# Seven block products in place of eight for the query, key and first feed-forward projections of a graph network layer

## The chip, the cores and the metric

The kernel runs on one NeuronCore of a Trainium2 chip. The metric is the device time of one launch in microseconds. Five engines of the core matter here: TensorE (PE in the profile, with PEld for its weight loads), VectorE (DVE), ScalarE (ACT), GpSimd (POOL) and SyncE (SP), which only issues DMAs. Each engine works through its own list of instructions in order and waits on semaphores for the others. Matrix products land in PSUM, which has eight banks of 512 float32 values per partition; everything else lies in SBUF.

## The reference

The input is x, 128 graphs of 64 nodes with 256 features, all in float32, and one 64x64 adjacency matrix. Four layers are added to x one after the other, each on a normalised copy of x with a ReLU. Layer 0 is a graph convolution followed by LSTMs over windows of 1 to 4 nodes. Layer 2 is graph attention, and layer 3 works in the eigenbasis of a graph Laplacian. Layer 1 is the one that the change touches:

```python
xp = jnp.einsum('mn,bnf->bmf', L_norm, x)
h = jax.nn.relu(_layernorm(xp @ Wc + bc, g1, be1))
x1 = h + x
q, k, v = x1 @ Wq, x1 @ Wk, x1 @ Wv          # 256 x 256 each, then split into 4 heads
attn = softmax(where(adjacency > 0, q @ k.T / sqrt(hd), -1e9))
o = (attn @ v) @ Wo + bo
x2 = _layernorm(x1 + o, g2, be2)
m = jax.nn.gelu(x2 @ W1 + b1) @ W2 + b2      # W1 is 256 x 512
return _layernorm(x2 + m, g3, be3)
```

(The listing is shortened: the reshapes into heads are left out.)

## The kernel before

The 8192 tokens (128 graphs of 64 nodes) are worked on as 64 tiles of 128 tokens. Layer 0 takes them in 8 groups of 8 tiles and writes its result to a buffer in HBM. Layers 1 to 3 take them in 16 groups of 4 tiles, so 512 tokens at a time: each group is fetched, goes through layer1, layer2 and layer3 (lines 1485, 1560, 1594), and is written to the output. Beside layer 0, an eigendecomposition of the 64x64 Laplacian runs, nearly all of it on VectorE.

The program text doesn't issue instructions. Every engine call is recorded by a planner (class Plan, lines 69 to 345), which sorts all recorded operations into one order by list scheduling on costs of its own, gives each value a buffer from a pool (36 "big" buffers of 1024 values per partition in the end, 8 PSUM banks, and smaller ones), and then issues everything from line 344. That is why every line of the profile says L344: instructions are told apart by the names of their tiles, which here are names of pools. In layers 1 to 3 "Wih" and "Whh" in a name are no LSTM weights: the room of LSTM weights that are done with is given to the weights of the later layers.

Three properties of the planner bear on the change. Groups overlap: up to 8 groups of layers 1 to 3 may be under way, and the operation of an older group mostly goes first; the last six groups count as one, and there the operation with the longest path behind it goes first (rank, line 328). A matrix product that depends on another engine is planned no earlier than 0.4 us after its inputs are expected (slack, line 976), 0.12 us for layer 0. VectorE's operations on SBUF alone and GpSimd's operations are planned never to overlap (the variable port in schedule, line 227). Dependences are taken from regions of a buffer, so two halves of a bank count as independent; the framework under it that inserts the semaphores decides for itself.

Weights of layers 1 to 3 are loaded once, as group WEIGHTS, when the last group of layer 0 lets go of the LSTM weights: a Carver (line 899) hands out the columns of these tiles first come, first served (lines 1390 to 1423).

In layer1, to_fm (line 1436) transposes x1 so that features lie on partitions: x1T is 128 partitions by 2 chunks of features by 512 tokens. proj_fm (line 1443) makes one half (128) of the output features of a projection: two products of 128x128 weights with 512 tokens, added up in one PSUM bank. Query and key take two calls each, W1 takes four. Their results are copied out of PSUM by evac (line 1430, VectorE for an even number, ScalarE for an odd one), and for W1 by ScalarE's Gelu with its bias. The value, Wc, Wo and W2 projections go through proj_tm (line 1449) and have 256 columns.

Products by seven block products exist already for the LSTM: pieces (line 1245) makes four differences of the blocks of the moving operand, the combinations of the weight blocks are prepared once (lines 1076 to 1088), and lstm_fast (line 1261) adds up the seven products with three PSUM banks.

Of the kernel before, what the change touches and what calls it, by code (L numbers as in the profile page):

```python
# [8 lines left out]
ALU = mybir.AluOpType  # L9
AF = mybir.ActivationFunctionType  # L10
# [877 lines left out]
P = 128  # L888
D = 256
# [3 lines left out]
HT = 4  # L893
# [39 lines left out]
def gnn_kernel(ctx: ExitStack, tc: tile.TileContext, a, out):  # L933
# [4 lines left out]
    def C(shape, name):  # L938
        return pool.tile(list(shape), F32, name=name)
# [3 lines left out]
    wih = [C([P, 2 * (3 if p == 0 else 4) * D], f"Wih{p}") for p in range(4)]  # L943
    whh = [None] + [C([P, 8 * D], f"Whh{p}") for p in range(1, 4)]
# [36 lines left out]
    plan = Plan(tc, {"PE": nc.tensor, "V": nc.vector, "ACT": nc.scalar, "G": nc.gpsimd, "SP": nc.sync}, pools, late, reserve, window, EIG, REST + NT // HT - 6, slack)  # L981
    PE, V, ACT, G, SP = (plan.proxy(e) for e in ("PE", "V", "ACT", "G", "SP"))

    def bank(name):
        return plan.value("bank")

    def load(t, src):
        SP.dma_start(t, src)
        return t

    def chunks(src):
        return src.rearrange("(c p) f -> p c f", p=P)
# [25 lines left out]
    Wg = [load(C([P, 2, D], f"Wg{i}"), chunks(a[f"Wg{i}"])) for i in range(2)]  # L1018
# [48 lines left out]
    B1T = C([P, 2, 2, P], "B1T")  # L1067
# [10 lines left out]
    for p in (1, 2):  # L1078
        fastw[p] = []
        for i, w in enumerate((Wih[p], Whh[p])):  # L1080
            a11, a12, a21, a22 = (w.rearrange("p k (q m n) -> p k q m n", q=4, m=2)[:, k, :, m, :] for m in range(2) for k in range(2))
            s1, s2, s4 = (space.tile([P, 4, P]) for j in range(3))
            s3 = a21 if i else space.tile([P, 4, P])
# [21 lines left out]
    room = Carver(arena)  # L1105
# [53 lines left out]
    flat = lambda t: t.rearrange("p t f -> p (t f)")  # L1159
# [21 lines left out]
    def fm():  # L1181

        return plan.value("big")[:, :2 * HT * P].rearrange("p (c n) -> p c n", c=2)
# [4 lines left out]
    def transposes(srcs):  # L1188

        pt = bank("tr")  # L1190
        for i, s in enumerate(srcs):
            PE.transpose(pt[:, i * P:(i + 1) * P], s, ident)
        return pt
# [51 lines left out]
    def pieces(B, eng):  # L1245

        n = B(0, 0).shape
        w = 1
        for k in n[1:]:
            w *= k  # L1250
        t = plan.value("big")[:, :4 * w].rearrange("p (i n) -> p i n", i=4)
        t = [t[:, i] for i in range(4)]
        if len(n) == 3:
            t = [v.rearrange("p (w t) -> p w t", t=n[2]) for v in t]
        eng.tensor_tensor(t[0], B(0, 1), B(0, 0), op=ALU.subtract)
        eng.tensor_tensor(t[1], B(1, 1), t[0], op=ALU.subtract)
        eng.tensor_tensor(t[2], B(1, 1), B(0, 1), op=ALU.subtract)
        eng.tensor_tensor(t[3], B(1, 0), t[1], op=ALU.subtract)
        return {1: B(0, 0), 2: B(1, 0), 3: B(1, 1), 4: t[3], 5: t[0], 6: t[1], 7: t[2]}
# [128 lines left out]


    plan.group = WEIGHTS  # L1390
    room = Carver(wih[1], whh[1], wih[2], whh[2], wih[0])
    wtile = lambda src: load(room.tile([P, src.shape[0] // P, src.shape[1]]), chunks(src))
    btile = lambda src, n=D: load(room.tile([P, n]), src.to_broadcast([P, n]))
    ctile = lambda shape, src: load(room.tile(shape), src)
    Wc, Wq, Wk, Wv, W1, W2, Wo = (wtile(a[n]) for n in ("Wc", "Wq", "Wk", "Wv", "W1", "W2", "Wo"))
    bc, g1, be1, bo, g2, be2, b2, g3, be3 = (btile(a[n]) for n in ("bc", "g1", "be1", "bo", "g2", "be2", "b2", "g3", "be3"))
    b1 = ctile([P, 4], a["b1"])

    g2c, be2c = (ctile([P, 2], a[n].rearrange("o (c p) -> p (o c)", p=P)) for n in ("g2", "be2"))
    G.tensor_tensor(b2, b2, be2, op=ALU.add)  # L1400
    W2a = wtile(a["L2_W"])

    wa = room.tile([P, 2, D])
    WT, a12 = fm(), wtile(a["L2_a"])
# [25 lines left out]
    def evac(dst, src, i):  # L1430
        if i % 2:
            ACT.copy(dst, src)
        else:
            V.tensor_copy(dst, src)
# [8 lines left out]
    def proj_fm(w, src, m):  # L1443
        ps = bank("fm")
        for c in range(2):
            PE.matmul(ps, w[:, c, tok(m)], src[:, c, :], start=c == 0, stop=c == 1)
        return ps

    def proj_tm(lhs, w, nk, t0):

        ps = bank("tm")
        for t in range(2):
            for c in range(nk):
                PE.matmul(ps[:, t * D:(t + 1) * D], lhs(c, t0 + t), w[:, c, :], start=c == 0, stop=c == nk - 1)
        return ps
# [29 lines left out]
    def layer1(x):  # L1485
        h = relu_norm(x)
        lx = mix_fm(h, lambda t: lapb)
        x1 = tm()
        for t0 in (0, 2):
            ps = proj_tm(lambda c, t: lx[:, c, tok(t)], Wc, 2, t0)  # L1490
            V.tensor_add(x1[:, t0:t0 + 2, :], ps.rearrange("p (t f) -> p t f", t=2), vec(bc, 2))
        norm(x1)
        for t0 in (0, 2):
            xp, hp = x1[:, t0:t0 + 2, :], h[:, t0:t0 + 2, :]
            V.tensor_mul(xp, xp, vec(g1, 2))
            G.tensor_add(xp, xp, vec(be1, 2))
            V.scalar_tensor_tensor(xp, xp, 0.0, hp, op0=ALU.max, op1=ALU.add)
        x1T = to_fm(x1)
        qT, kT, v = fm(), fm(), tm()
        for m in range(2):  # L1500
            evac(qT[:, m, :], proj_fm(Wq, x1T, m), 0)
            evac(kT[:, m, :], proj_fm(Wk, x1T, m), 1)
        for t0 in (0, 2):
            evac(pair(v, t0), proj_tm(lambda c, t: x1T[:, c, tok(t)], Wv, 2, t0), 1)
        for t0 in (0, 2):
            G.tensor_add(x1[:, t0:t0 + 2, :], x1[:, t0:t0 + 2, :], vec(bo, 2))


        ps = [bank("qk") for m in range(2)]
        with plan.burst():  # L1510
            for b, m, r in [(b, m, r) for b in range(2 * HT) for m in range(2) for r in range(2)]:
                PE.matmul(ps[m][half(r ^ m), bat(b)], qT[half(r), m, bat(b)], kT[half(r), m, bat(b)], start=True, stop=True)
        s = tm(4 * HT, N)
        for m in range(2):
            sm = s[:, m * 2 * HT:(m + 1) * 2 * HT, :]
            V.scalar_tensor_tensor(sm, ps[m].rearrange("p (b k) -> p b k", k=N), 0.125, vec(mask1, 2 * HT), op0=ALU.mult, op1=ALU.add)
            stat = plan.value("stat")
            softmax_shift(sm, stat[:, :2 * HT])
            ACT.activation(sm, sm, AF.Exp)
            ssum = stat[:, 2 * HT:4 * HT]  # L1520
            V.reduce_sum(ssum, sm, axis=AX.X)
            V.reciprocal(ssum, ssum)
            G.tensor_mul(sm, sm, ssum.unsqueeze(2).to_broadcast([P, 2 * HT, N]))

        pT = fm()
        for m in range(2):
            evac(pT[:, m, :], transposes([flat(s[:, (m * HT + t) * 2:(m * HT + t) * 2 + 2, :]) for t in range(HT)]), m)
        oT = fm()

        po = [bank("o") for i in range(2)]  # L1530
        with plan.burst():
            for m, t, i, r in [(m, t, i, r) for m in range(2) for t in range(HT) for i in range(2) for r in range(2)]:
                PE.matmul(po[i][half(r), bat(m * HT + t)], v[half(i), t, bat(2 * m + r)], pT[half(i), m, bat(2 * t + (r ^ m))], start=True, stop=True)
        for i in range(2):
            evac(oT.rearrange("p c (t b n) -> p c t b n", t=HT, b=2)[:, :, :, i, :], po[i].rearrange("p (c t n) -> p c t n", c=2, t=HT), i)
        x2 = tm()
        for t0 in (0, 2):
            ps = proj_tm(lambda c, t: oT[:, c, tok(t)], Wo, 2, t0)
            V.tensor_add(x2[:, t0:t0 + 2, :], ps.rearrange("p (t f) -> p t f", t=2), x1[:, t0:t0 + 2, :])
        norm(x2)  # L1540
        x2T = fm()
        for c in range(2):
            ACT.activation(x2T[:, c, :], transposes([x2[:, t, tok(c)] for t in range(HT)]), AF.Identity, scale=g2c[:, c:c + 1], bias=be2c[:, c:c + 1])
        V.tensor_mul(x2, x2, vec(g2))
        for t0 in (0, 2):
            G.tensor_add(x2[:, t0:t0 + 2, :], x2[:, t0:t0 + 2, :], vec(b2, 2))
        mT = [fm() for i in range(2)]
        for m in range(4):
            ACT.activation(mT[m // 2][:, m % 2, :], proj_fm(W1, x2T, m), AF.Gelu, bias=b1[:, m:m + 1])
        for t0 in (0, 2):  # L1550
            ps = proj_tm(lambda c, t: mT[c // 2][:, c % 2, tok(t)], W2, 4, t0)
            V.tensor_add(pair(x2, t0), ps, pair(x2, t0))
        for t0 in (0, 2):
            G.tensor_add(x[:, t0:t0 + 2, :], x[:, t0:t0 + 2, :], vec(be3, 2))
        norm(x2)
        for t0 in (0, 2):
            V.tensor_mul(x2[:, t0:t0 + 2, :], x2[:, t0:t0 + 2, :], vec(g3, 2))
            V.tensor_add(x[:, t0:t0 + 2, :], x[:, t0:t0 + 2, :], x2[:, t0:t0 + 2, :])
# [115 lines left out]
```

## Time and profile before

| | us |
|---|---|
| median of 3 runs (lowest, highest) | 2162.17 (2159.51, 2166.93) |
| the profiled execution: time | 2164.86 |
| the profiled execution: span from first to last instruction | 2163.1 |
| PE busy | 2117.6 (98%) |
| DVE busy | 1795.0 (83%) |
| ACT busy | 1066.5 (49%) |
| POOL busy | 650.6 (30%) |

The span is 1.8 us shorter than the time of its own execution, which in turn is 2.7 us above the median. Busy time is the union of an engine's instructions. For PE a float32 product of the program stands as two MATMUL records with two LDWEIGHTS records, and a record's own duration is longer than the distance from its start to the next one's, since they are pipelined: for the cost of a product one reads the distance. "[3.99 <-DMA x]" behind an instruction says that its engine was idle 3.99 us before it and that a DMA into x ended the wait. The layer 0 stage ends at about 1320 us; what follows is layers 1 to 3.

### The profile page before, as it was taken

To read this page: it belongs to the slowest core of one execution; us is meant where nothing else is said; L and a number is where in the kernel's file an instruction comes from. 1 tells how busy PE (TensorE), PEld (TensorE's weight loads), DVE (VectorE), ACT (ScalarE), POOL (GpSimd) and SP (SyncE) were. 2 spreads that over 40 slices of the span, in tenths; PEclk is the share of its full clock that TensorE was granted. 3 is DMA by queue.
4 is the path that set the end of the run, shared out by engine and by line. 5 is a ranking of instruction groups with operands and counts; after the bars stand their busy time and mean duration, and the time that the engine had idled before them with its cause. 6 is when DMAs were issued, how large, how long until landed. Compare 5 with 4: busy or idle time off the path is not lost. (4 is left out here: it accounts for less than half of the span.)

```text
span 2163.1 us, 45587 instructions
## 1 busy us (share of the span) xinstructions
PE 2117.6 (98%) x16580; PEld 1632.8 (75%) x16580; DVE 1795.0 (83%) x7402; ACT 1066.5 (49%) x2321; POOL 650.6 (30%) x968
## 2 busy tenths in 40 slices
PE   9999999999999999999999999999999999999997
PEld 6688688688678688678778788767677777676776
DVE  5788888888899999889989887777887778875796
ACT  3354354354344344345345343555556656545673
POOL 7211221210200110110110101675456555644353
PEclk9999999999999999999999999999999999999999
DMA  5000100100100100100000111200010000000001
GB/s 205 1 3 22 41 3 21 40 1 21 40 1 20 40 1 20 40 1 20 26 1 21 52 44 44 89 1 21 1 41 21 22 21 21 11 21 2 1 2 60
DMA packets 44865, 57.66 MB, mean 27 GB/s; under 512 B 8928, under 2 KB 38496, under 8 KB 44640
## 3 DMA queue, kind: packets, MB, share of 16 engines
q1 hardware_dynamic: 43536, 53.71, 7.5%
q8 instruction: 130, 2.13, 0.4%
q10 hardware_dynamic: 1104, 1.05, 0.2%
q14 instruction: 95, 0.78, 0.1%
HBM read 37.53 MB, written 16.78 MB: 25 GB/s over the span
## 5 line engine op out<-in xcount | busy, mean ns | idle before, releaser
L344 PE MATMUL bank<-big,Wih 128*128 128x256 f32 (+3 forms) x2400 | 751.8, 436 | 14.4 <-DVE arena L344 6.7
L344 PEld LDWEIGHTS bank<-big,Wih 128*128 128x128 f32 x2400 | 440.3, 191 | 194.0 <-issue 112.1
L344 ACT ACTIVATE mids<-bank,bl 128x256 f32<-128x256 f32 (+3 forms) x528 | 274.6, 526 | 387.5 <-PE bank L344 385.3
L344 PE MATMUL bank<-big,Whh 128*128 128x256 f32 (+2 forms) x1624 | 431.5, 367 | 3.7 <-DVE big L344 3.7
L344 DVE TENSOR_TENSOR arena<-arena 64x21 f32<-64x21 f32 (+5 forms) x2251 | 372.1, 195 | 29.8 <-POOL arena L344 1.3
L344 PEld LDWEIGHTS bank<-big,Whh 128*128 128x128 f32 x1624 | 294.1, 190 | 42.8 <-issue 9.9
L344 PE MATMUL bank<-big,sums 128*128 128x168 f32 (+2 forms) x1664 | 267.5, 310 | 0.3
L344 POOL TENSOR_SCALAR stat<-stat 128x4 f32<-128x4 f32 (+1 forms) x228 | 71.1, 313 | 561.8 <-DVE stat L344 547.9
L344 PEld LDWEIGHTS bank<-big,sums 128*128 128x128 f32 (+1 forms) x1664 | 223.6, 179 | 17.2 <-issue 4.5
L344 ACT COPY mids<-bank 128x168 f32<-128x168 f32 (+2 forms) x378 | 124.8, 349 | 147.7 <-PE bank L344 142.9
L344 DVE TENSOR_TENSOR big<-mids 128x512 f32<-128x512 f32 (+2 forms) x256 | 141.8, 563 | 36.1 <-ACT mids L344 32.9
L344 ACT ACTIVATE mids<-mids,bl 128x336 f32<-128x336 f32 (+3 forms) x192 | 102.0, 539 | 77.6 <-DVE mids L344 73.6
L344 DVE SCALAR_TENSOR_TENSOR arena<-arena 64x1 f32<-64x1 f32 (+15 forms) x565 | 122.3, 239 | 6.2 <-POOL arena L344 2.5
L344 POOL TENSOR_TENSOR stat<-stat,mhalf 128x4 f32<-128x4 f32 (+1 forms) x114 | 121.9, 1070 | 6.4
L344 ACT ACTIVATE mids<-big 128x256 f32<-128x256 f32 (+2 forms) x176 | 89.4, 510 | 67.6 <-DVE big L344 48.0
L344 DVE TENSOR_TENSOR mids<-bank,mids 128x168 f32<-128x168 f32 (+1 forms) x294 | 103.1, 356 | 8.4 <-PE bank L344 4.7
L344 DVE TENSOR_SCALAR arena<-arena 64x1 f32<-64x1 f32 (+8 forms) x533 | 103.1, 200 | 8.4 <-POOL arena L344 0.4
L344 DVE TENSOR_TENSOR big<-big,mids 128x256 f32<-128x256 f32 (+2 forms) x192 | 93.7, 488 | 11.0 <-ACT mids L344 10.0
L344 POOL TENSOR_TENSOR big<-big 128x168 f32<-128x168 f32 (+1 forms) x24 | 15.8, 671 | 262.0 <-DVE arena L344 135.8
L344 POOL TENSOR_TENSOR arena<-arena 64x1 f32<-64x1 f32 x66 | 44.8, 678 | 152.6 <-ACT arena L344 106.3
L344 DVE BATCH_NORM_STATS2 stat<-big 128x6 f32<-128x256 f32 x228 | 83.2, 406 | 4.9 <-DMA big<-put 4.0
L344 ACT COPY big<-bank 128x512 f32<-128x512 f32 x90 | 49.5, 586 | 58.0 <-PE bank L344 55.9
(366 smaller groups left out, 3663.0 us busy)
## 6 DMA issues: line engine op xcount, KB each, us to landing
big<-in_x_dram SPq DMA_DIRECT2D x30, 512.0 KB, 5.3
put<-big SPq DMA_DIRECT2D x16, 512.0 KB, 2.8
arena<-put SPq DMA_DIRECT2D x8, 512.0 KB, 6.8
out_dram<-arena SPq DMA_DIRECT2D x16, 256.0 KB, 2.2
big<-put SPq DMA_DIRECT2D x7, 512.0 KB, 4.4
out_dram<-big SPq DMA_DIRECT2D x14, 256.0 KB, 2.4
Wih<-in_WihT_dram SPq DMA_DIRECT2D x3, 1024.0 KB, 12.1
Whh<-in_WhhT_dram SPq DMA_DIRECT2D x3, 1024.0 KB, 13.8
```

The lines of the kernel that those rows point to most:

```text
L344: getattr(self.engines[op.eng], name)(*map(real, args), **{k: real(a) for k, a in kw.items()})
```

## The change

The query, key and the two halves of the W1 projection are each a 256x256 matrix times 256 features by 512 tokens. Each is cut into 2x2 blocks, 128x128 of weights and 128x256 of tokens, and made by seven block products (Winograd's form of Strassen's algorithm) where the block form has eight.

- Once, among the weights: lefts makes four combinations of each of the four weight matrices on GpSimd, 16 operations of 128x128. Twelve new tiles of 128 columns come from the Carver, ahead of the weights of layers 2 and 3, which move to other places; the rooms of Wg and B1T are added to it.
- Per group of 512 tokens: pieces makes four differences of the blocks of x1T, and four of x2T, on GpSimd, in a further "big" buffer.
- proj_fast takes the place of two calls of proj_fm. It uses two banks. Bank a adds up product 1, then 6, 7 and 4, and is read by ScalarE or VectorE after each step; the other bank holds product 2 in its first half and products 5 and 3 in its second. Query and key end with a copy, W1 with Gelu on three pieces.
- Two other evacuations, of the transposed attention weights (pT) and of the attention's output (oT), of which VectorE and ScalarE made one half each, all go to ScalarE.

```diff
-    room = Carver(wih[1], whh[1], wih[2], whh[2], wih[0])
+    room = Carver(wih[1], whh[1], wih[2], whh[2], wih[0], *(w.rearrange('p c f -> p (c f)') for w in Wg), B1T.rearrange('p a b c -> p (a b c)'))
...
     G.tensor_tensor(b2, b2, be2, op=ALU.add)
+
+    def lefts(w):
+        a11, a12, a21, a22 = (w[:, k, m * P:(m + 1) * P] for m in range(2) for k in range(2))
+        s1, s2, s4 = (room.tile([P, P]) for j in range(3))
+        s3 = a21
+        G.tensor_tensor(s1, a21, a22, op=ALU.add)
+        G.tensor_tensor(s2, s1, a11, op=ALU.subtract)
+        G.tensor_tensor(s3, a11, a21, op=ALU.subtract)
+        G.tensor_tensor(s4, a12, s2, op=ALU.subtract)
+        return {1: a11, 2: a12, 3: s4, 4: a22, 5: s1, 6: s2, 7: s3}
+
+    fastp = {"Wq": lefts(Wq), "Wk": lefts(Wk)}
+    fastp["W1"] = [lefts(W1[:, :, i * D:(i + 1) * D]) for i in range(2)]
     W2a = wtile(a["L2_W"])
...
+    def proj_fast(L, R, dst, fn=None, bias=None):
+
+        w = HT * P // 2
+        a, b = bank("fast"), bank("fast")
+
+        a, c, b = a[:, :w], b[:, :w], b[:, w:2 * w]
+        lo, hi = ([dst[:, m, n * w:(n + 1) * w] for n in range(2)] for m in range(2))
+
+        def prod(ps, i, start=False):
+
+            PE.matmul(ps, L[i], R[i], start=start, stop=True, skip_group_check=True)
+        with plan.burst(3 * (0.001672 * w + 0.006)):
+            prod(a, 1, True)
+            prod(c, 2, True)
+            prod(b, 5, True)
+        ACT.copy(lo[0], a)
+        ACT.copy(hi[1], b)
+        V.tensor_tensor(lo[0], c, lo[0], op=ALU.add)
+        prod(a, 6)
+        ACT.copy(lo[1], a)
+        prod(b, 3)
+        V.tensor_tensor(lo[1], b, lo[1], op=ALU.add)
+        prod(a, 7)
+        V.tensor_tensor(hi[1], a, hi[1], op=ALU.add)
+        prod(a, 4)
+        if fn:
+            ACT.activation(dst[:, 0, :], dst[:, 0, :], fn, bias=bias(0))
+            ACT.activation(hi[0], a, fn, bias=bias(1))
+            ACT.activation(hi[1], hi[1], fn, bias=bias(1))
+        else:
+            ACT.copy(hi[0], a)
...
         qT, kT, v = fm(), fm(), tm()
-        for m in range(2):
-            evac(qT[:, m, :], proj_fm(Wq, x1T, m), 0)
-            evac(kT[:, m, :], proj_fm(Wk, x1T, m), 1)
+        R = pieces(lambda c, n: x1T[:, c, n * HT * P // 2:(n + 1) * HT * P // 2], G)
+        proj_fast(fastp["Wq"], R, qT)
+        proj_fast(fastp["Wk"], R, kT)
...
-            evac(pT[:, m, :], transposes([flat(s[:, (m * HT + t) * 2:(m * HT + t) * 2 + 2, :]) for t in range(HT)]), m)
+            evac(pT[:, m, :], transposes([flat(s[:, (m * HT + t) * 2:(m * HT + t) * 2 + 2, :]) for t in range(HT)]), 1)
...
-            evac(oT.rearrange("p c (t b n) -> p c t b n", t=HT, b=2)[:, :, :, i, :], po[i].rearrange("p (c t n) -> p c t n", c=2, t=HT), i)
+            evac(oT.rearrange("p c (t b n) -> p c t b n", t=HT, b=2)[:, :, :, i, :], po[i].rearrange("p (c t n) -> p c t n", c=2, t=HT), 1)
...
-        for m in range(4):
-            ACT.activation(mT[m // 2][:, m % 2, :], proj_fm(W1, x2T, m), AF.Gelu, bias=b1[:, m:m + 1])
+        R = pieces(lambda c, n: x2T[:, c, n * HT * P // 2:(n + 1) * HT * P // 2], G)
+        for i in range(2):
+            proj_fast(fastp["W1"][i], R, mT[i], AF.Gelu, lambda m: b1[:, 2 * i + m:2 * i + m + 1])
```

## The prediction

> **What bounds the kernel.** I read the totals of the page first, then the busy time by stretches of the stage that layer 1 lies in, then what TensorE waited for there.
>
> ```profile
> PE 2117.6 (98%) x16580; PEld 1632.8 (75%) x16580; DVE 1795.0 (83%) x7402; ACT 1066.5 (49%) x2321; POOL 650.6 (30%) x968
> ```
>
> The stretches have, behind their length, the busy time of PE, PEld, DVE, ACT and POOL:
>
> ```profile
> 1320.00:1500.00 180.00, 174.95 (x1803) 134.69 (x1803) 136.78 (x410) 92.31 (x175) 103.66 (x129) 0.98 0.08 28
> 1500.00:1700.00 200.00, 199.38 (x2054) 146.84 (x2053) 159.73 (x464) 118.60 (x212) 111.92 (x152) 1.00 0.07 23
> 1700.00:1900.00 200.00, 196.06 (x2118) 143.98 (x2117) 158.64 (x448) 118.62 (x209) 110.80 (x148) 1.00 0.07 23
> 1913.00:2101.00 188.00, 187.85 (x1743) 136.03 (x1741) 140.56 (x396) 111.52 (x187) 85.90 (x121) 1.00 0.01 4
> 2101.00:2163.10 62.10, 49.29 (x811) 40.93 (x809) 44.72 (x138) 26.65 (x52) 22.15 (x34) 0.95 0.16 53
> ```
>
> PE is full from 1500 to 2101 us; the others have room (DVE 75 to 80%, ACT 59%, POOL 46 to 56%). Only the last 62 us, where six groups end together, leave PE 13 us idle. From 1320 us on the whole list of PE's waits is 17.8 us long, its largest entries these (total us, times, longest):
>
> ```profile
> PE bank L344 <- DVE arena L344: 4.1, 8, 0.9
> PE bank L344 <- ACT arena L344: 4.0, 3, 1.5
> ```
>
> So PE work taken out of this stage should shorten it, if no new waits come in. The price of a product is read from the timeline, where a row starts with its start and its length:
>
> ```profile
> 1321.18 1.03 PE L344 MATMUL bank<-big,Wih 128*128 128x256 f32 x4
> ...
> 1925.51 6.17 PE L344 MATMUL bank<-arena,Wih 128*128 128x512 f32 x14
> ```
>
> The last record of a row counts with its full length (0.38 and 0.60 us, the means of the two shapes), the others with their distance: (1.03 - 0.38) / 3 = 0.217 us for 256 columns and (6.17 - 0.60) / 13 = 0.428 us for 512. A product is two records: 0.433 and 0.857 us. Narrower products cost next to nothing extra, and their weight loads (0.19 us) fit into 0.217 us.
>
> [...] a VectorE operation on 512 columns of SBUF takes 0.68 us alone and more beside GpSimd:
>
> ```profile
> 1925.91 2.49 POOL L344 TENSOR_TENSOR sums<-sums,stat 128x512 f32<-128x512 f32 x2 [0.55 <-DVE stat L344]
> ...
> 1926.43 1.07 DVE L344 TENSOR_TENSOR big<-big,Wih 128x512 f32<-128x512 f32 x1
> ...
> 1927.42 1.53 DVE L344 SCALAR_TENSOR_TENSOR big<-big,arena 128x512 f32<-128x512 f32 x1
> ```
>
> [...]
>
> **PE.** Per group of 512 tokens the four projections have 16 products of 512 columns, 16 x 0.857 = 13.71 us; afterwards 28 of 256, 28 x 0.433 = 12.13 us. The difference is 1.58 us, by 16 groups **25.4 us**. The bounds come from other runs of records: 0.215 us (four records start between 1560.02 and 1560.88) gives 26.7, 0.2196 us (28 records in 6.31 us at 1309) gives 22.6.
>
> **New waits of PE.** Products 6 and 7 wait for ScalarE to read bank a, 4 for VectorE, 3 for ScalarE to read b[...]. That is 4 waits by 4 projections by 16 groups, 256. PE is in order: a late one holds everything behind it, other groups' products included. Before has the same pattern in the LSTM, with 3 such waits per gate, 4 gates, 3 steps and 8 groups, 288 in all, and less slack. From 100 to 1300 us PE waited there, in all:
>
> ```profile
> PE bank L344 <- DVE arena L344: 6.9, 7, 1.4
> PE bank L344 <- DVE big L344: 3.1, 2, 2.2
> PE bank L344 <- ACT mids L344: 2.7, 1, 2.7
> PE bank L344 <- DVE mids L344: 1.2, 2, 0.9
> ```
>
> The two rows of "mids", the tiles of that pattern, are 3.9 us: 0.014 us for each wait. All four rows together, 13.9 us, would be 0.05. I take 0.03, since ACT is busier here: 256 x 0.03 = **7.7 us** lost (3.6 to 12.8; at 0.1 us each, 25.6).
>
> **DVE, ACT and POOL, per group.** DVE loses four evacuations of 512 columns (0.68 us each) and gains twelve additions of 256 (0.417): +2.3 us. ACT loses two copies (0.585) and four Gelu (0.715), and gains fourteen copies of 256 (0.376, the LSTM's), two Gelu on 512 from SBUF (0.72), four on 256 (0.47 to 0.51) and two copies of 512: +5.8 us. POOL gains eight operations of 256 columns at 0.70: +5.6 us. A group takes PE about 807.5 / 16 = 50 us from 1320 on (a little less, as the first part still holds layer 0), hence about 48.5 afterwards. DVE goes from 80% to about 87%, ACT from 59 to 73%, POOL from 55 to 68%. All stay under PE, and PE's work on the other groups hides them. Without that cover, in the last 62 us, they would cost their own length; but layer 1 of the last groups is over by then, as its last Gelu starts at 2088. What may reach the end is the extra DVE work of the six last groups, 14 us, against 47 us of idle DVE between 1913 and 2101; I put it at **1 us** (0 to 5).
>
> **The weights.** 16 operations on POOL, at most 0.67 us each (its row at 168 columns), so 5 to 11 us, between 1250 and 1325, where POOL waits for most of the time; twelve of the sixteen must wait until a tile of the last LSTM is free, at about 1303. The query needs them after 1325, so nothing is lost unless they delay the first norms: up to 3 us. On the other side a wait goes. SP loads nb3a and W2a after the LSTM's end today, behind ten other loads, and DVE stands before nb3a:
>
> ```profile
> 1316.93 0.23 DVE L344 TENSOR_SCALAR Whh<-Whh 128x128 f32<-128x128 f32 x1 [3.99 <-DMA Whh<-in_L_b_dram]
> ...
> 1318.03 0.70 PE L344 MATMUL bank<-big,Whh 128*128 128x256 f32 x2 [2.61 <-DVE big L344]
> ```
>
> Counting columns through the Carver, nb3a, W2a and wa now fall into Wih0, and W3a, W3b, b3b and C3 into Wih0's remainder or Wg, all free earlier; two small loads (a12, b3a) stay where they were and could be waited for instead. Between -3 and +3 us; I take **0**. SP gets no DMA more per group, and the fetches depend on free "big" buffers: one more is held by each projection stage, of 36.
>
> **Sum.** 2164.9 (the profiled execution's time) - 25.4 + 7.7 + 1 + 0 = 2148.2 us. The profiled execution is 2.7 us above the median of the runs, so against 2162.2 I predict **2145 us**.
>
> **Rivals.**
> 1. *Everything arrives* (0.08): waits as cheap as the LSTM's (3.6), the 26.7 us in full, the nb3a wait gone: 2162.2 - 26.7 + 3.6 - 2.6 = 2136.5; some planning luck beside it gives 2133 or so.
> 2. *The load moves to DVE[...]* (0.22). If POOL's 16 x 5.6 = 90 us hold VectorE off for half their time, DVE has 45 us more to do and 93% to carry, and a late DVE is a late product 4. For it speaks the 1.53 us operation above; against it that PE shows so few DVE waits today with DVE at 80%. Two thirds of the gain goes: about 2154.
> 3. *Slower: PE stands behind the partial sums* (0.12). Each of the 256 waits runs against a copy of 0.376 us that the planner prices at 0.28, with ACT at 73%[...]. At 0.099 us per wait (25.4 / 256) the gain is gone, at 0.125 the kernel is measurably slower, at 0.18 it takes 2162 - 25.4 + 46 = 2183. Against it: planned slack of 0.4 us per product, and the LSTM's 0.014.
> 4. *No effect* (0.03): the last six groups' chain of DVE work sets the end whatever PE saves, and waits eat the rest: 2162.
>
> The rest, 0.55, is the forecast with 2135 to 2155. A difference under 0.3% (6.5 us) can't be told from none here. Rival 2 straddles that line, and I give 0.14 of it to faster: **faster** 0.55 + 0.08 + 0.14 = 0.77; **same** 0.08 + 0.03 = 0.11; **slower** 0.12. The range that leaves out rival 3's slow end and the luckiest cases is **2133 to 2166**; its upper end is 0.1 us per wait and 5 us at the end.
>
> **What would show it.** PE records go from 16580 to 16964 (896 of 256 columns for 512 of 512), PE busy from 2117.6 to about 2092 us. DVE should count about 7530, POOL 1112, ACT 2577 apart from table loads, of which there are 37 after 1320 us and may be ten more. The step of the waits is right if PE's waits from 1320 us on are near 25 us and none of their rows is longer than 10; it is wrong if rows of ACT or DVE on "bank" hold 30 us or more, and then rival 3 is at work. Rival 2 shows as DVE above 90% between 1500 and 2100 with long SBUF operations. If the end grows, the last stretch with idle PE is longer than 62 us. I would be wrong altogether if PE's busy time fell as said and the span didn't.

## The result, and the profile after

| | before | after |
|---|---|---|
| median (lowest, highest), us | 2162.57 (2159.51, 2166.93) | 2183.88 (2179.75, 2184.77) |
| ratio to before, 95% interval | | 1.0089 (1.0076 to 1.0102) |
| the profiled execution: time / span, us | 2164.86 / 2163.1 | 2184.77 / 2183.0 |
| from 1320 us to the end: length, us | 843.1 | 863.0 |
| from 1320 us to the end: PE busy, us | 820.3 | 809.1 |
| from 1320 us to the end: PE idle (length less busy), us | 22.8 | 53.9 |

(The median of before is over its runs beside the changed kernel, hence 2162.57.) The changed kernel is 21 us slower; 2145 us were predicted. First the totals of its page:

```profile
span 2183.0 us, 46901 instructions
...
PE 2107.7 (97%) x16964; PEld 1712.3 (78%) x16964; DVE 1839.3 (84%) x7530; ACT 1137.6 (52%) x2571; POOL 766.1 (35%) x1112
```

The instructions are there as counted: 16964 PE records, 7530 on DVE, 1112 on POOL, and on ACT the 256 more that the count has, beside ScalarE's loads of function tables, of which there are 33 where before had 39. But PE's busy time fell by 9.9 us where 25 were due, and the span rose by 19.9. Busy time by stretches, with the columns of the prediction (length, then PE, PEld, DVE, ACT, POOL, then the granted clock):

```profile
1320.00:1500.00 180.00, 170.23 (x1577) 146.59 (x1576) 130.60 (x405) 103.20 (x216) 115.91 (x146) 0.96 0.08 28
1500.00:1700.00 200.00, 194.22 (x2356) 166.12 (x2355) 179.12 (x516) 135.07 (x274) 139.83 (x184) 1.00 0.08 23
1700.00:1900.00 200.00, 186.16 (x2252) 158.36 (x2251) 163.36 (x450) 128.37 (x256) 139.71 (x182) 0.97 0.07 20
1900.00:2108.00 208.00, 200.99 (x1898) 171.12 (x1897) 161.53 (x463) 143.57 (x283) 121.34 (x165) 1.00 0.02 7
2108.00:2183.00 75.00, 57.49 (x990) 47.64 (x988) 53.45 (x165) 31.47 (x60) 27.49 (x42) 0.95 0.13 44
```

PE, which was full from 1500 to 2101 us, now idles in every stretch: 9.8, 5.8, 13.8, 7.0 and 17.5 us. The other engines are not full either (from 1500 to 1900 us DVE has 86%, ACT 66%, POOL 70%), so no single one of them is busy enough to be the bound. PE's waits after 1320 us (total us, times, longest):

```profile
PE bank L344 <- DVE arena L344: 8.1, 11, 1.9
PE bank L344 <- ACT sums L344: 6.4, 6, 3.1
PE bank L344 <- ACT big L344: 6.3, 7, 2.7
PE bank L344 <- ACT mids L344: 6.3, 3, 4.3
PE bank L344 <- DVE big L344: 4.9, 6, 2.2
PE bank L344 <- ACT arena L344: 4.4, 4, 1.2
```

The loss is few and long waits spread over many places, not many short ones at one: the row of "ACT mids" is 6.3 us in three waits. The stretches also show a clock below 1.00. Here are four windows around one long wait, and PE's own timeline from the end of the wait on (start, length, and the idle time before it in brackets):

```profile
1380.00:1392.00 12.00, 11.33 (x248) 9.48 (x240) 11.71 (x42) 7.88 (x16) 11.59 (x22) 1.00 0.01 3
1391.00:1394.20 3.20, 0.88 (x31) 0.47 (x20) 1.25 (x3) 3.17 (x6) 3.20 (x3) 1.00 0.00 0
1394.20:1401.00 6.80, 5.83 (x51) 4.81 (x52) 5.09 (x15) 4.32 (x9) 5.76 (x6) 0.50 0.01 2
1402.00:1410.00 8.00, 8.00 (x102) 6.86 (x102) 3.82 (x12) 5.07 (x11) 6.59 (x10) 1.00 0.01 3
```

```profile
1395.17 1.35 PE L344 MATMUL bank<-lapb,sums 64*64 64x64 f32 x40 [3.09 <-ACT sums L344]
1396.45 5.09 PE L344 MATMUL bank<-Wih,sums 128*128 128x256 f32 x12
```

PE waits 3.09 us, and runs at half clock for 6.8 us from shortly before the end of the wait on: twelve records take 5.09 us, about 0.42 each, where 0.217 is the price at full clock. After 1320 us the changed kernel has 31.1 us at half clock, before had 12.9. Half of that is lost at most, 15.5 against 6.5 us; counting only the time in which PE was busy there (26.7 and 8.6 us), it is 13.4 against 4.3. The difference is 9.1 us either way.

So the balance of the stage from 1320 us, which grew by 19.9 us, is: products -25.4 (the predicted price), idle PE +31.1, half clock +9.1. That leaves +5.1. The distances between starts show some 5 us more in gaps of up to 0.16 us, which lie under the tails of the records (one of 256 columns is 0.38 us long, at a distance of 0.217) and count as busy.

### The profile page after: what moved, and what is told of

Its sections match the earlier page's. It is cut to its first block, busy times and chain, and to the rows that moved or that the text cites. A ratio compares the mean times of both kernels' runs of the same rounds, so it can differ in the third digit from the quotient of the medians.

```text
span 2183.0 us, 46901 instructions
## 1 busy us (share of the span) xinstructions
PE 2107.7 (97%) x16964; PEld 1712.3 (78%) x16964; DVE 1839.3 (84%) x7530; ACT 1137.6 (52%) x2571; POOL 766.1 (35%) x1112
## 4 chain that ended last, share of the span: by engine, by line
PE 77%; DVE 15%; ACT 3%; POOL 2%; DMA 2%; issue 2%; SPq 0%; ACTq 0%; DVEq 0%; POOLq 0%
PE bank L344 77%; DVE stat L344 4%; DVE arena L344 4%; DVE big L344 4%; DVE sums L344 1%; DVE mids L344 1%; POOL stat L344 1%; DMA big<-in_x_dram 1%; ACT arena L344 1%; ACT mids L344 1%; ACT big L344 1%; POOL arena L344 1%; ACT sums L344 0%; SPq L344 0%; POOL big L344 0%
## 5 line engine op out<-in xcount | busy, mean ns | idle before, releaser
L344 PE MATMUL bank<-big,Wih 128*128 128x256 f32 (+3 forms) x2418 | 736.9, 426 | 15.5 <-DVE arena L344 6.9
L344 PE MATMUL bank<-big,Whh 128*128 128x256 f32 (+1 forms) x1738 | 448.5, 358 | 3.1 <-DVE big L344 1.0
L344 PEld LDWEIGHTS bank<-big,Whh 128*128 128x128 f32 x1738 | 315.3, 190 | 35.9 <-ACT sums L344 1.4
L344 ACT COPY mids<-bank 128x256 f32<-128x256 f32 (+2 forms) x453 | 156.8, 364 | 175.2 <-PE bank L344 168.7
L344 PEld LDWEIGHTS bank<-big,sums 128*128 128x128 f32 (+1 forms) x1600 | 222.6, 181 | 16.1 <-issue 3.4
L344 DVE TENSOR_TENSOR mids<-bank,mids 128x168 f32<-128x168 f32 (+2 forms) x345 | 125.3, 370 | 35.4 <-PE bank L344 22.2
L344 POOL TENSOR_TENSOR big<-big 128x168 f32<-128x168 f32 (+1 forms) x28 | 20.3, 736 | 270.2 <-DVE arena L344 105.7
L344 POOL TENSOR_TENSOR arena<-arena 64x1 f32<-64x1 f32 (+1 forms) x74 | 51.2, 692 | 152.1 <-ACT arena L344 108.6
L344 ACT COPY big<-bank 128x512 f32<-128x512 f32 (+1 forms) x163 | 73.8, 476 | 55.4 <-PE bank L344 54.0
L344 POOL MEMSET arena<- 64x2 f32 (+5 forms) x72 | 7.7, 112 | 208.6 <-DVE arena L344 208.6
```

The source lines that it names most:

```text
L344: getattr(self.engines[op.eng], name)(*map(real, args), **{k: real(a) for k, a in kw.items()})
```

## The experiments

My theory after the traces: **the order**. The planner does not keep the order and exchange some products. It sorts all operations of layers 1 to 3 anew, on its own costs, and the new order leaves PE without ready work now and then. If so, time should move as much when only the order is changed and no work at all. The rivals were **the partial sums** (PE stands before products 3, 4, 6 and 7 of a projection; rival 3 of the prediction) and **the side changes** (weights moved, evacuations all on ScalarE). In the expectations on record A is the order, B the partial sums and C the side changes; the later theories are told where they come. A new order also means another choice of buffers from the pools, and the two are not told apart here. "Planned end" below is the end of the schedule that the program works out for itself before it issues anything: planned by its own costs, not a time of the chip. The changed kernel has 2153.3, before 2144.8. So 8.5 of the 20 us are already in the schedule, although its planned PE work is 26.3 us less.

### Parts of the change

`old_products` has the side changes but the old products. The combinations of weights are still made, s3 in a room of its own so that the weights stay whole, and the pieces are not. The edit is against the changed kernel, as in all diffs here but that of the rule for VectorE and GpSimd, which is the same line in both:

```diff
-        s1, s2, s4 = (room.tile([P, P]) for j in range(3))
-        s3 = a21
+        s1, s2, s4, s3 = (room.tile([P, P]) for j in range(4))
...
-        proj_fast(fastp["Wq"], R, qT)
-        proj_fast(fastp["Wk"], R, kT)
+        for m in range(2):
+            evac(qT[:, m, :], proj_fm(Wq, x1T, m), 0)
+            evac(kT[:, m, :], proj_fm(Wk, x1T, m), 1)
...
+        for m in range(4):
+            ACT.activation(mT[m // 2][:, m % 2, :], proj_fm(W1, x2T, m), AF.Gelu, bias=b1[:, m:m + 1])
```

> The changed kernel with all four projections put back to eight block products by two calls each; the combined weights are still made (into tiles of their own), the weights keep their new places, the evacuations of pT and oT stay on ScalarE. Theory A: the planner's schedule is 2147.3 us, so about 2167. Theory B: 2162, since the partial sums are gone. Theory C: 2184, since all that it blames is still there.

Measured: 2160.32 us (2157.13 to 2162.11), ratio 0.9981 (0.9972 to 0.9990). The side changes cost nothing, so theory C falls. Theory A missed too: it had 2167 us, because the planned end (2147.3) is 2.5 us longer than that of before. The DMA wait of 3.99 us that stood before the VectorE operation at 1316 us has no successor: from 1300 to 1350 us PE is idle for 1.1 us in the changed kernel, 1.3 us in this one and 4.2 us before.

`qk_only` has the seven products for query and key, and leaves W1 with eight:

```diff
-        R = pieces(lambda c, n: x2T[:, c, n * HT * P // 2:(n + 1) * HT * P // 2], G)
-        for i in range(2):
-            proj_fast(fastp["W1"][i], R, mT[i], AF.Gelu, lambda m: b1[:, 2 * i + m:2 * i + m + 1])
+        for m in range(4):
+            ACT.activation(mT[m // 2][:, m % 2, :], proj_fm(W1, x2T, m), AF.Gelu, bias=b1[:, m:m + 1])
```

> The changed kernel with the W1 projection put back to eight block products; query and key stay at seven, the evacuations stay on ScalarE. PE's work is half of the change's: -12.7 us. Theory A: the planner's schedule is 2137.8 us, and with a lag of execution between those of before (18) and after (30) the time is about 2164. Theory B: half of the loss, about 2173. Theory C: 2184 or a little less.

Measured: 2153.28 us (2152.61 to 2154.69), ratio 0.9952 (0.9937 to 0.9967). Half of the change gains 9.7 us, with half of the partial sums in it. That is near its half of the predicted PE work (12.7), but this is no price of the half: its planned end (2137.8) is 7.0 us shorter than that of before, so it is one draw of the order too, and theory A had 2164 us. From 1320 us:

```profile
1320.00:2150.80 830.80, 804.81 (x8869) 642.74 (x8868) 645.55 (x1891) 528.05 (x983) 487.53 (x650) 1.00 0.07 22
```

PE's idle time is 26.0 us, hardly more than before. If each partial sum cost in any order what the full change lost by it, half of it could not have gained.

### The order alone

The only edit is the planner's slack for products of layers 1 to 3, in the changed kernel or in the one before. No operation of the program is added or left out; only ScalarE's table loads depend on the order (43 with 0.6, 33 with 0.4 in the changed kernel).

```diff
-            return 0.4 if op.group >= REST and op.group != EIG else 0.12
+            return 0.6 if op.group >= REST and op.group != EIG else 0.12
```

> The changed kernel with one number of the planner altered: a product of layers 1 to 3 is planned no earlier than 0.6 us after its inputs, in place of 0.4. Same instructions, another order. Theory A (the loss lies in the order that the planner finds: it leaves PE without ready work): the planner's own schedule has 2137.1 us here against 2153.3 for the changed kernel, so the time falls with it, to about 2169 us (16 below the changed kernel). Theory B (PE stands behind the partial sums of the seven-product projections themselves, as rival 3 had it): the products and their waits are the same, so 2178 to 2184. Theory C (the side changes: evacuations on ScalarE, combined weights, places of the weights): 2184.

> The kernel before with the same number at 0.3 us in place of 0.4. Theory A: the planner's schedule is 2150.1 us against 2144.8 for the kernel before, so about 5 us slower than before, 2168. Theories B and C: nothing that they speak of is in this kernel, 2162.

Measured: the changed kernel with 0.6 takes **2147.47 us** (2146.29 to 2148.30), ratio 0.9924 (0.9909 to 0.9938), the one before with 0.3 takes 2179.12 us (2177.25 to 2181.17), ratio 1.0070 (1.0055 to 1.0085). The same work in another order moves the changed kernel by 36 us and the one before by 16. Theory A has the direction of both right and the size too small: it had 2169 and 2168 us, since the planned ends move by only 16.2 and 5.3 us. The changed kernel with 0.6 beats both kernels. Its totals and its stage from 1320 us:

```profile
PE 2092.3 (98%) x16964; PEld 1702.7 (79%) x16964; DVE 1841.8 (86%) x7530; ACT 1143.8 (53%) x2581; POOL 762.4 (36%) x1112
```

```profile
1320.00:2144.90 824.90, 793.82 (x9068) 680.76 (x9066) 690.88 (x1994) 548.92 (x1099) 541.60 (x716) 1.00 0.07 22
```

PE is busy for 2092.3 us, idle for 31.1 us from 1320 on, and never at half clock there. Its longest rows of waits are short now:

```profile
PE bank L344 <- DVE arena L344: 6.5, 10, 1.3
PE bank L344 <- DVE sums L344: 2.8, 4, 1.1
```

Whether slack 0.6 is simply the better setting, and 0.4 a lucky one for before, was asked by filling the grid.

> The kernel before with the planner's 0.6 us for a product in place of 0.4, the pair of the run of the changed kernel at 0.6. Theory A (the time follows the order that the planner draws): its schedule has 2148.4 us, and at 0.6 execution lagged 8 us behind the schedule, so about 2160. Theory G (there is a gain of about 25 us, and 0.4 is a bad draw for the changed kernel alone): 2172, 25 above the changed kernel's 2147.5. Theory L (the kernel before at 0.4 is the lucky draw, every other is slower): 2165 to 2180.

> The changed kernel at 0.3 us, the pair of the kernel before at 0.3 (2179.1). Theory A: the planner's schedule has 2146.1 us, the lag at 0.3 was 26 us, so about 2174. Theory G: 2154, 25 below its pair. Theory B (the partial sums cost more than they save in any order but a lucky one): 2195 to 2200, 16 to 21 above its pair.

> The changed kernel at 0.5 us. Theory A: the planner's schedule has 2155.3 us, with a lag of 10 to 20 us the time is 2167 to 2177, above the kernel before at 0.5. Theory G: 25 below its pair. Theory B: 16 to 21 above its pair.

> The kernel before at 0.5 us. Theory A: the planner's schedule has 2152.8 us, with the same lag 2165 to 2175. Theory L: 2165 to 2180, above the 2163 of the kernel before at 0.4. If 0.4 is an ordinary draw for the kernel before, 2160 to 2165.

| slack | before, us | after, us | difference | planned difference | PE idle from 1320: before, after | half of the time at half clock: before, after |
|---|---|---|---|---|---|---|
| 0.3 | 2179.1 | 2170.3 | -8.8 | -4.0 | 30.5, 45.4 | 3.2, 8.8 |
| 0.4 | 2162.6 | 2183.9 | +21.3 | +8.5 | 22.8, 53.9 | 6.5, 15.5 |
| 0.5 | 2170.2 | 2174.6 | +4.5 | +2.5 | 28.4, 49.3 | 2.8, 8.5 |
| 0.6 | 2162.7 | 2147.5 | -15.2 | -11.3 | 24.4, 31.1 | 1.7, 0.0 |
| mean | 2168.6 | 2169.1 | +0.5 | -1.1 | 26.5, 44.9 | 3.5, 8.2 |

(The two columns of times are medians; idle and clock are from the profiled executions; the planned difference is the difference of the planned ends.) Three things follow.

- The effect of the same change runs from -15.2 to +21.3 us with the setting. The theory that the changed kernel has one constant gain or loss, and the setting an effect of its own, falls. With 0.4 the comparison met before at one of its two best settings and the changed kernel at its worst.
- The sign stands in the schedule each time: the measured difference follows the planned one and is 1.3 to 2.5 times as large. (A small difference can be lost: the old products are planned 2.5 us longer than before and were measured 2.6 us shorter than it.) The spans are 8 to 30 us longer than planned, and the slack shows there, before first: 26 and 23 us with 0.3, 18 and 30 with 0.4, 16 and 18 with 0.5, 8 and 8 with 0.6. With the most slack, 0.6, the chip fell behind the least.
- The mean over the four is +0.5 us. With a spread of 16 us between four settings its standard error is 8 us, and a 95% interval from four values reaches from about -25 to +26 us. So whether the change gains on average, by the predicted 17 us say, stays open. The idle column is clearer: PE's idle time grew at every setting, by 6.7 to 31.1 us, on average by 18.4, and the last column by 4.7.

The partial sums themselves can be counted by laying the program's order of products beside their records in the trace. After 1320 us the list of PE's waits (gaps over 0.15 us) is 48.3 us long after the change and 17.8 before it. Of the growth of 30.5 us, 11.9 us (12 waits) stand right before a product 3, 4, 6 or 7 of the new projections. The rest stands before products, transposes and mixes of any kind, of other groups too, such as the mix at 1395 us above. Over the four settings the list grew by 15.1, 30.5, 20.6 and 5.8 us, of which 3.1, 11.9, 7.4 and 4.6 us are partial sums: 6.7 of 18.0 us on average. So the partial sums are part of the loss, somewhat over a third of the new waits, and what they cost depends on the order. Two of the four longest waits at 0.4 are among them, before a product 7 at 1471 us and a product 4 at 1853 us:

```profile
1471.51 2.05 PE L344 MATMUL bank<-arena,Wih 128*128 128x256 f32 x4 [4.28 <-ACT mids L344]
...
1853.58 0.67 PE L344 MATMUL bank<-arena,Wih 128*128 128x256 f32 x2 [2.17 <-DVE big L344]
1854.09 0.59 PE L344 MATMUL bank<-Wih,big 128*128 128x256 f32 x2
1854.52 0.60 PE L344 MATMUL bank<-sums,same 128*128 128x256 f32 x2
1854.95 2.73 PE L344 MATMUL bank<-arena,Wih 128*128 128x256 f32 x6
```

At 1853 us PE stood 2.17 us for one operation of VectorE, the reading of bank a, and the list had no product of another group to fill the time with; then six records took 2.73 us instead of 1.5.

### Less work for GpSimd

The change gives GpSimd 6.6 us more per group (105.8 us from 1320 on, by 16), and the planner never lets it overlap VectorE's work on SBUF. To see whether this eats the gain, both kernels were run with most of GpSimd's work in the stage taken away:

```diff
-            G.tensor_add(xp, xp, vec(be1, 2))
...
-            G.tensor_add(x1[:, t0:t0 + 2, :], x1[:, t0:t0 + 2, :], vec(bo, 2))
...
-        R = pieces(lambda c, n: x1T[:, c, n * HT * P // 2:(n + 1) * HT * P // 2], G)
+        R = plain(x1T)
```

The additions of b2, be3 and b3b and the pieces of x2T go likewise. plain hands the blocks of x1T to the products as they are, in place of the differences, so the seven products stay with the same shapes. The kernel before loses the five additions alone.

> The kernel before with less GpSimd work: it leaves out the five additions of bias vectors on GpSimd in layers 1 and 3 (be1, bo, b2 with be2, be3, b3b; ten operations of 512 columns per group; with these inputs the vectors are zero). Planner at 0.4 us. The planner's schedule has 2146.9 us against 2144.8 with the additions. Theory P (GpSimd, and the planner's rule that it never works beside VectorE on SBUF, takes the change's gain): nothing here, since PE bounds this kernel, 2160 to 2170. Theory Q (the gain goes elsewhere, to PSUM banks and evacuations): the same.

> The changed kernel without the same five additions and without the differences that pieces makes: the seven products take plain blocks of tokens, so query, key and W1 projections have other values than the reference's. All products, evacuations and banks are as in the changed kernel. Planner at 0.4 us. Theory P: the seven products now pay; the planner's schedule has 2134.2 us, the time is 2146 to 2160 and 10 to 20 below the light kernel before. Theory Q: no gain over the light kernel before beyond the scatter of orders, 2160 to 2180.

> The light kernel before at the planner's 0.6 us, as a second pair. The planner's schedule has 2151.0 us; with the lag of 8 us seen at 0.6, about 2161 under both theories.

> The light changed kernel at 0.6 us. Theory P: the planner's schedule has 2131.4 us, the time is about 2141, 20 below its pair. Theory Q: the full kernels differ by 15 at this setting; the light ones then differ by no more than that, 2147 or above.

| slack | before, light | after, light | difference | difference of the full kernels | PE idle from 1320, light |
|---|---|---|---|---|---|
| 0.4 | 2160.56 | 2153.15 | -7.4 | +21.3 | 23.8, 35.0 |
| 0.6 | 2162.74 | 2144.54 | -18.2 | -15.2 | 24.8, 31.5 |

(Ratios to the kernel before: 0.9984, 0.9953, 0.9994, 0.9908, each within 0.0017.) The expectations call it P that GpSimd takes the gain, and Q that it goes elsewhere. The kernel before gains little from a lighter GpSimd, the changed one 31 us at 0.4 and 3 at 0.6. Theory P had 10 to 20 us between the light kernels at 0.4, where 7.4 were measured, and 20 at 0.6, where it was 18.2. But the lighter kernels are new draws of the order too: the light changed kernel is planned 12.7 and 19.6 us shorter than the light kernel before. In the light pair the change is worth 12.8 us on average, against -3.1 at the same two settings in full. So GpSimd's work seems to take part of the gain, but at two settings the spread (28.7 and 3.0 us) is as large as the effect: how large a part stays open. PE's idle time still grows by 9 us (18.9 in the full kernels at these settings) with GpSimd at 27% (226.61 of 831.00 us), so it is not the whole:

```profile
1320.00:2151.00 831.00, 795.98 (x9065) 681.96 (x9063) 647.84 (x1990) 544.14 (x1096) 226.61 (x429) 1.00 0.07 22
```

Is the planner's rule for the two engines needed at all? Without it the planner takes VectorE and GpSimd for independent. The planned end of the changed kernel is shorter then (2137.6 for 2153.3), that of the kernel before longer (2156.4 for 2144.8).

```diff
-                    t = max(now[e], op.ready, port) if op.port else max(now[e], op.ready)
+                    t = max(now[e], op.ready)
```

> The changed kernel, planner at 0.4 us, without the rule that GpSimd's operations and VectorE's on SBUF are planned one after the other. The same instructions in another order; the planner's schedule has 2137.6 us against 2153.3. Theory P1 (the rule takes the gain, the chip's own conflict is small): 2150 to 2160. Theory P2 (the conflict is the chip's): the schedule is wrong about it, execution lags by 35 us or more, and the time is 2175 or above.

> The kernel before without the same rule, planner at 0.4 us; the planner's schedule has 2156.4 us against 2144.8. Theory P1: a lag of 10 to 20 us and 2168 to 2178. Theory P2: 2180 or above.

Measured: 2263.01 us (ratio 1.0455, 1.0439 to 1.0472) and 2249.63 us (1.0398, 1.0380 to 1.0416): 79 us more than the changed kernel takes with the rule, 87 more than before does. The chip runs 125 and 92 us behind the planned ends. VectorE's 7530 operations are the same, and yet in the changed kernel its busy time grew from 1839.3 to 1880.3 us, while GpSimd's went from 766.1 to 761.0:

```profile
PE 2138.1 (95%) x16964; PEld 1712.0 (76%) x16964; DVE 1880.3 (83%) x7530; ACT 1133.5 (50%) x2573; POOL 761.0 (34%) x1112
```

So VectorE's same operations took 41.0 us longer on the chip without the rule, and both kernels were faster with it. The 79 and 87 us are more than any change of the order alone made here, but a new order is in them as well. PE's waits in the whole of the changed kernel without the rule:

```profile
PE bank L344 <- DVE arena L344: 37.3, 28, 10.2
PE bank L344 <- DVE big L344: 21.3, 28, 2.6
```

### A bank more for each projection

The last suspect was the shared bank: product 2 lies beside products 5 and 3, and the framework under the planner may let one half wait for the other, a suspicion of mine that no trace showed. With a third bank they are apart, at the price of a bank taken from the other groups.

```diff
-        a, b = bank("fast"), bank("fast")
+        a, b, c = bank("fast"), bank("fast"), bank("fast")
-        a, c, b = a[:, :w], b[:, :w], b[:, w:2 * w]
+        a, c, b = a[:, :w], c[:, :w], b[:, :w]
```

> The changed kernel, planner at 0.6 us, with products 2 and 5 in two PSUM banks of their own, so three banks per projection in place of two. Theory K (PSUM banks are short once projections hold them for so long): the planner's schedule has 2189.4 us against 2137.1 with two banks, the time is about 2199, 50 above. Theory H (the bank that products 2, 5 and 3 share makes PE and VectorE wait for each other, which the planner doesn't know): a bank each removes this, 2140 to 2147.

> The same at 0.5 us, where the planner's schedule has 2142.3 us against 2155.3 with two banks. If the time follows the schedule whatever the number of banks, about 2160, below the 2174.6 of two banks; if banks are short at every setting (theory K in its strong form), above 2175.

Measured: 2197.76 us with slack 0.6 (2195.41 to 2201.88), ratio 1.0163 (1.0143 to 1.0182), and 2153.73 with 0.5 (2151.06 to 2156.36), ratio 0.9953 (0.9935 to 0.9971). Against two banks that is +50.3 at 0.6 and -20.9 us at 0.5; the planned ends moved by +52.3 (2137.1 to 2189.4) and -13.0 (2155.3 to 2142.3). Neither "a bank more ends such waits" nor "a bank less for the others costs" holds at both; the schedule does, though the run at 0.5 came out 6 us below the 2160 that were expected from it. In the slow one a single kind of wait tells:

```profile
PE bank L344 <- ACT Wih L344: 16.1, 3, 7.4
PE bank L344 <- DVE sums L344: 9.7, 10, 1.8
```

Three waits make 16.1 us: an order with a few bad places.

### The planner alone

Since the schedule carries the sign, I also looked at planned ends by themselves, over 12 settings (slack 0.2 to 0.5, weight of a group's age 5 to 7). Before has a mean of 2154.0 us (standard deviation 4.2), after 2152.4 (4.3), with 26.3 us less planned PE work. The planner itself can turn hardly any of it into a shorter schedule. The setting as it was (2144.8) is the shortest of the twelve for before. With two banks more than there are, the changed kernel's mean falls to 2142.3, without the rule for VectorE and GpSimd to 2141.2, with both to 2127.8; before stays within 1 us with either (rule 2154.5, banks 2154.6) and has 2145.4 with both. So in the planner's eyes much of the saved time is held up by PSUM banks and by the rule for VectorE and GpSimd, both of which the change loads more. These are the planner's costs, not times of the chip: the program has its eight banks, without the rule the chip took 79 and 87 us more, and this part is argued, not shown.

## Why the prediction was wrong

**PE, -25.4 us: the price was right.** The records came as counted, and from 1320 us on the starts of records at full clock lie 0.216 us apart for 256 columns and 0.429 for 512 (medians after and before), which makes it 26 us. That PE's busy time of 2092.3 us at 0.6 meets the 2092 predicted is partly luck, as the kernel before has less at 0.6 too, and the difference is 18.2 us:

```profile
PE 2110.5 (98%) x16580; PEld 1629.7 (76%) x16580; DVE 1800.9 (84%) x7402; ACT 1070.3 (50%) x2323; POOL 658.4 (31%) x968
```

**DVE, ACT and POOL, per group: near.** From 1320 us on they grew by 38.3, 68.8 and 105.8 us, so by 2.4, 4.3 and 6.6 us per group for the 2.3, 5.8 and 5.6 predicted. Six table loads fewer, where ten more were thought possible, are part of ACT's difference. DVE came to 86% between 1500 and 1900 us for 87.

**"All stay under PE, and PE's work on the other groups hides them": this is the step that failed.** It took the cover that PE has in the trace of before, with 5 us idle in 601, as a property of the kernel. It is one of the order: PE was so full because the list of before happens to hold a ready product at nearly every point. The change threw that list away, and with the new one the cover has holes: +31.1 us idle at 0.4, +18.4 on average over four settings, the smaller part of it before partial sums. The Sum had no term for idle time before any other product, and none for the clock (9.1 us at 0.4). I had described the planner and then priced the change as if the order around it stayed.

**New waits of PE, 7.7 us (3.6 to 12.8): low at 0.4, near on average.** The 256 waits measured 11.9 us in the list of waits, 0.046 us each, and some 14 by the distances between starts, which show short gaps too. Over the four settings it is 3.1 to 11.9 us in the list, 6.7 on average. That is part of the loss, but it alone would not have cost the gain of 25.4 us.

**The end, 1 us (0 to 5): within its bounds.** PE's idle time in the last stretch went from 12.8 us (62 us long) to 17.5 (75 us). **The weights, 0: right,** within its 3 us, as the old products with moved weights show (-2.6 us against the runs of before beside them, with everything beside the products changed).

**The rivals.** Rival 3 gave the time, 2183 us, by luck: its mechanism occurred, but it needed 0.18 us per wait, and even 0.099 to lose the gain, where 0.046 were measured. By the limits that I set in advance, the step of the waits is wrong: the list is 48.3 us long where near 25 was the limit, and the six rows shown of ACT and DVE hold 36.4 us, over 30. That verdict is right, but the second half of it, "then rival 3 is at work", is right for 11.9 of the 48.3 us only. A loss spread over products of all kinds was on no list. Rival 2's sign, DVE above 90% between 1500 and 2100 us, is absent (504.00 of 608 us, 83%), while the planner's rule for VectorE and GpSimd does matter: without it the kernels took 79 and 87 us more. In Rival 1 I had "some planning luck", worth some 3 us and only on the good side.

**How the numbers follow.** The range of 2133 to 2166 held only uncertainties of prices. Another order without any change of work moves the kernel before by 16 us, and the changed one by 36. The trace of one order could not show that, but "sorts all recorded operations into one order" stood in front of me. A spread of some 15 us to either side belonged into the range, and most of the certainty about the sign should have gone.

## What to carry to other kernels

Where a list scheduler orders the instructions, an edit draws a new order, and one pair of timings compares two draws. Vary a setting that changes the order but no work (here 16 to 36 us) before pricing an edit worth 25, and search that setting again after the edit: 0.6 in place of 0.4 makes the changed kernel 2147.5 us, faster than both. PE was 98% busy here thanks to its order. Work taken from such an engine is a gain only in an order in which the others can hand it products that much faster, so look at what they and the shared buffers have to take on.

## What the hardware showed that I had not expected

PE's clock halves after waits shorter than I thought mattered: in the changed kernel it is 0.50 for 6.8 us after the wait of 3.09 us at 1395 us and for 3.4 us after the one of 2.17 at 1853. In the 3.4 us ahead of the second stretch, PE was busy for 1.23:

```profile
1851.40:1854.80 3.40, 1.23 (x7) 1.12 (x7) 3.40 (x6) 1.03 (x3) 1.16 (x1) 1.00 0.02 5
1855.00:1858.40 3.40, 3.40 (x10) 2.68 (x9) 2.72 (x10) 1.10 (x3) 1.34 (x2) 0.50 0.01 2
```

A wait of 2.17 us thus cost 1.7 us on top of itself. In this trace all four waits of PE above 2 us after 1320 us (2.17, 2.65, 3.09 and 4.28) go with a stretch at half clock, of 3.4 or 6.8 us, and none of the thirteen of 0.97 to 1.87 us before 2140 us has one of its own. The kernel before shows the same after a wait of 2.57 us at 1382 us, but also at 1412.9 us after five waits of 0.16 to 0.66 us in a row. The clock records of the two kernels' traces show more of it. In each trace they all start on one grid of 3.413 us, to within 0.004 us (18 records after, 12 before). Of the stretches of this grid at full clock, all 8 in which the profile has PE busy for less than 1.41 us were followed by one at half clock, and none of the 1209 with more than 2.25 us; between the two, 7 of 31 were. So in these traces the half clock goes with how little PE did within one stretch of the grid, and not with one wait's length: the wait of 1.87 us at 1826 left PE 1.56 us of work in its stretch, and the clock stayed. With slack 0.6, where PE's longest wait is 1.5 us, there is no half clock from 1320 us to the last instruction.

That VectorE's operations on SBUF take longer beside GpSimd was known to the prediction as a price of single operations. In the trace of before, from 1320 us on, the 60 of its TENSOR_TENSOR operations of 128x512 on SBUF that had no GpSimd instruction beside them took 0.68 us on average, and the 67 that had one 0.90, the longest 1.76. What this is worth for a whole schedule was not known: taking the planner's rule for it away costs 79 to 87 us, with 41.0 us more of busy VectorE in the changed kernel.
